# Last pair's experts summed per chosen token on the chip and put out by plain scatters; later expert groups take all images

## The chip, the cores and the metric

The kernel runs on one core of a Trainium2 chip. The metric is the device time of one execution in microseconds (us), lower is better. Engines are named as the profile names them: PE (TensorE, matmul), DVE (VectorE), ACT (ScalarE), POOL (GpSimd), SP (SyncE, which only issues DMAs here). A name with a q ("SPq") is the queue of that engine.

## What is computed

Two layers of a network over 32 images of 56 x 56 tokens with 128 channels: a binarized 3 x 3 convolution and a two-of-eight mixture of experts, then a triangle product and a second expert layer. The change lies in this second expert layer, in which every one of 64 experts chooses 8 tokens of each image:

```python
def _L1_ffn_ref(x, gate_w, gate_b, weight1, weight2):      # x: (32, 3136, 128), layer-normed tokens
    logits = jnp.einsum('bsd,ed->bse', x, gate_w) + gate_b
    probs = jax.nn.softmax(logits, axis=1)                 # over the tokens of an image
    vals, idx = jax.lax.top_k(probs.transpose(0, 2, 1), K) # 8 tokens per expert
    ...
    pooled = jnp.einsum('bked,bke->bed', gathered, topv)
    ...
    h = jax.nn.gelu(jnp.einsum('ebd,edh->ebh', h, weight1), approximate=False)
    ...
    out = jnp.einsum('ebh,eho->ebo', h, weight2)
    out = out.transpose(1, 0, 2)
    weighted = jnp.einsum('beo,bke->bkeo', out, topv).reshape(Bn, K * E, O)
    outputs = jnp.zeros((Bn, Sn, O), dtype=x.dtype)
    outputs = outputs.at[jnp.arange(Bn)[:, None], flat_idx].add(weighted)
    return outputs
# main:  x = x + triangle(ln(x));  t = tokens(x);  t = t + _L1_ffn_ref(_ln_t(t), ...)
```

A token may be chosen by several experts of its image, so the additions of different experts can fall on the same row.

## The kernel before

A first pass over x takes the statistics of the batch norm. The main loop then goes over 16 pairs of images, in 7 units of 896 tokens per pair; pairs overlap. The last stages of a pair are: `tri_out` (the triangle's output added to the tokens `x_`), `gate_turn` (L1045: the finished tokens go to `out` by a DMA from ACT's queue, their norm `yl` to DRAM as `y3_d` by another), `gate_logits`, `top8` (L1090: the eight best tokens per expert, their numbers `near` within the pair and in `pg` within the whole output, their weights in the other half of `pg`, and eight gathers of rows of `y3_d` by POOL) and `pool_rows` (L1141: the weighted sum of the eight rows per expert and image, transposed into `ptc`; for pairs 0 to 14 it goes to `pooled_d` in DRAM; numbers and weights go through DRAM into the tables `picked` and `gains`, one row per image and rank).

The expert matmuls follow when the pooled rows are there, in 16 groups of four experts. `late_experts(last, g)` (L1216) is called twice for each group: with False for pairs 0 to 14 and with True for the last pair, since its pooled rows come latest. A call loads a group's weights (eight loads of 256 KB at L1284 and L1288 and four bias loads of 64 KB at L1239, from SP's queue), and computes all 32 columns of tokens with those of the other pairs at zero: `ph` (first matmul), `hs` (DVE adds the bias), `trh` (transposes), `hG` (ACT, Gelu), `po` (second matmul), a copy by ACT into `oS`, then for each lot `pe` (each image's row repeated eight times by a matmul with `rep`, bias added) and `eo` (DVE, times `gains`, L1358). Then POOL adds it to `out`, one indirect DMA per expert with addition in the DMA (L1375). Lots are images 0 to 15, 16 to 29, 30 to 31; within a lot each of these DMAs waits for the one before it to land, since both may add to the same token, and different lots are declared to be apart. That makes 64 dependent scatters for each of three lots.

Buffers: weights of the experts take turns in the tag `gb` (5 tiles) and in `x` (12 tiles, which also hold tokens and `oS`), `eo` in `xT` (4) for False and `yl` (3) for True, `hs` and `hG` in `u` (5).

The order of the work is not the program's: each stage records operations with an engine, a cost, what it reads and writes, and a rank (the tick in the plan at the end), and `Order.run` (L132) plays them in a model of the engines and writes the instructions of every engine in the order this gave. An engine then takes its instructions strictly in that order, so an instruction that waits holds everything behind it on its engine, DMA issues too.

Of the kernel before, what the change touches and what calls it, by code (L numbers as in the profile page):

```python
# [253 lines left out]
def kernel(ctx: ExitStack, tc: tile.TileContext, a: dict, out: bass.AP):  # L254
# [82 lines left out]


    LOTS = ((0, HB), (HB, B - 2), (B - 2, B))
    picked = [const.tile([HB * K1, E1], I32, name=f"picked_{k}") for k in range(3)]  # L340
    gains = [const.tile([HB * K1, E1], F32, name=f"gains_{k}") for k in range(3)]

    between = const.tile([1, 1], F32, name="between")
    rep = const.tile([B + 1, B * K1], F32, name="rep")
# [24 lines left out]
    with ExitStack() as c2:  # L369
# [35 lines left out]
        def parts(t, n=N7):  # L405
            return [(t, k) for k in range(n)]
# [638 lines left out]
        def gate_turn(p, u):  # L1045

            x_ = live[p]["x", u]

            @op("ACT", 330, r=parts(x_), w=[("out", p, u)], land=1200)
            def _():  # L1050
                ins = nc.scalar.dma_start(out_units[p * NU + u], x_.ap).ins
                apart(ins, lot_of(p))
                stored[lot_of(p)].append(ins.name)

            y = normed(p, u, "ln4", f"yl_{p}_{u}")

            @op("ACT", 330, r=parts(y), w=[("y3", p, u)], land=1200)
            def _():
                nc.scalar.dma_start(units(y3_d[p])[u], y.ap)

            live[p]["yl", u] = copied(turned(y, f"trl_{p}_{u}"), "yl", f"ylT_{p}_{u}")
# [28 lines left out]
        def top8(p):  # L1090

            lg = live[p].pop("lg")
            m8 = new("m8", [2 * E1, K1], f"m8_{p}")
            i8 = new("i8", [2 * E1, K1], f"i8_{p}", U32)
            q = new("sq", [2 * E1, 3], f"sq_{p}")
            pg = live[p]["pg"] = new("pg", [2 * E1, 2 * K1], f"pg_{p}")
            near = new("near", [2 * E1, K1], f"near_{p}", I32)
            all_lg = [(lg, k, i) for k in range(7) for i in range(2)]

            @op("DVE", 3400, r=all_lg, w=[m8])  # L1100
            def _():
                nc.vector.max(m8.ap, lg.ap)

            @op("DVE", 3600, r=all_lg + [m8], w=[i8, q, near, (pg, 0)])
            def _():
                nc.vector.max_index(i8.ap, m8.ap, lg.ap)
                nc.vector.tensor_scalar(q.ap[:, 0:1], m8.ap[:, 0:1], -1.0, None, ALU.mult)
                nc.vector.tensor_scalar(near.ap, i8.ap, row0, None, ALU.add)

                nc.vector.tensor_scalar(  # L1110
                    pg.ap[:, :K1], i8.ap, row0, float(2 * p * S), ALU.add, ALU.add
                )

            @op("ACT", 2700, r=[q, m8], w=all_lg + [(q, 1), (pg, 1)])
            def _():
                nc.scalar.activation(
                    pg.ap[:, K1:], m8.ap, AF.Exp, bias=q.ap[:, 0:1]
                )
                nc.scalar.activation(
                    lg.ap, lg.ap, AF.Exp, bias=q.ap[:, 0:1], accum_out=q.ap[:, 1:2]  # L1120
                )

            @op("DVE", 300, r=[(q, 1), (pg, 1)], w=[(pg, 2)])
            def _():
                nc.vector.reciprocal(q.ap[:, 2:3], q.ap[:, 1:2])
                nc.vector.tensor_scalar(pg.ap[:, K1:], pg.ap[:, K1:], q.ap[:, 2:3], None, ALU.mult)

            for k in range(0, K1, 4):
                rows = live[p]["rows", k // 4] = new("u", [2 * E1, 4, C], f"rows_{p}_{k}")
                for j in range(4):  # L1130
                    @op("POOL", 1300, r=[near] + [("y3", p, u) for u in range(NU)],
                        w=[(rows, j)], land=2600)
                    def _(rows=rows, j=j, k=k):
                        nc.gpsimd.indirect_dma_start(  # L1134
                            out=rows.ap[:, j, :], out_offset=None, in_=y3_d[p],
                            in_offset=bass.IndirectOffsetOnAxis(
                                ap=near.ap[:, k + j : k + j + 1], axis=0
                            ),
                        )

        def pool_rows(p):  # L1141

            pg = live[p]["pg"]
            acc = new("pacc", [2 * E1, C], f"acc_{p}")
            for k in range(K1):
                rows = live[p]["rows", k // 4]

                @op("DVE", 265, r=[(rows, k % 4), (pg, 2)], w=[acc])
                def _(k=k, rows=rows):
                    row, g = rows.ap[:, k % 4, :], pg.ap[:, K1 + k : K1 + k + 1]  # L1150
                    if k == 0:
                        nc.vector.tensor_scalar(acc.ap, row, g, None, ALU.mult)
                    else:
                        nc.vector.scalar_tensor_tensor(
                            acc.ap, row, g, acc.ap, ALU.mult, ALU.add
                        )

            tr = bank(f"tr_p_{p}")
            pt = new("ptc", [C, E1, 2], f"ptc_{p}")
            pk = new("pt", [2 * K1, 2 * E1], f"pt_{p}")  # L1160

            @op("PE", 220, r=[acc, (pg, 0), (pg, 2)], w=[tr])
            def _():
                nc.tensor.transpose(tr.ap[:, :128], acc.ap, ident)
                nc.tensor.transpose(tr.ap[: 2 * K1, 128:256], pg.ap, ident)

            @op("ACT", 300, r=[tr], w=[pt, pk])
            def _():

                nc.scalar.copy(  # L1170
                    pt.ap.rearrange("c e i -> c i e"),
                    tr.ap[:, :128].rearrange("c (i e) -> c i e", i=2),
                )
                nc.scalar.copy(pk.ap, tr.ap[: 2 * K1, 128:256])

            @op("DVE", 100, r=[pk], w=[pk])
            def _():
                nc.vector.tensor_copy(pk.ap[:K1].bitcast(I32), pk.ap[:K1])

            @op("SP", 720, r=[pk], w=[("pick", p)], land=300)  # L1180
            def _():
                for k0, dst, as_ in ((0, pick_d[p], I32), (K1, gain_d[p], F32)):
                    nc.sync.dma_start(
                        dst.rearrange("i k e -> k i e"),
                        pk.ap[k0 : k0 + K1, :].bitcast(as_).rearrange("k (i e) -> k i e", i=2),
                    )

            lot = lot_of(p)

            @op("SP", 720, r=[("pick", p)], w=[("picked", p)], land=300)  # L1190
            def _():
                r0 = (2 * p - LOTS[lot][0]) * K1
                for dst, src in ((picked, pick_d), (gains, gain_d)):
                    nc.sync.dma_start(
                        dst[lot][r0 : r0 + 2 * K1, :], src[p].rearrange("i k e -> (i k) e")
                    )

            if lot == 2:
                live[p]["pt"] = pt
                return  # L1200

            @op("SP", 360, r=[pt], w=[("pooled", p)], land=1500)
            def _():
                nc.sync.dma_start(
                    pooled_d[:, :, p, :], pt.ap.rearrange("c (g e) i -> c g (e i)", e=NE)
                )
# [3 lines left out]

        tokens_out = out.rearrange("b h w c -> (b h w) c")
        last_out = {}

        def late_experts(last, g):  # L1216

            name = f"{last}_{g}"
            es = slice(g * NE, (g + 1) * NE)
            n = (NP - 1) * NE * 2  # L1220

# [23 lines left out]
                    a["L1_ffn_weight2"][es, HID, :].unsqueeze(0),  # L1245
                )

            if last:
                pt = live[NP - 1]["pt"]

                @op("DVE", 250, r=[pt], w=[(oS, "t")])
                def _():
                    nc.vector.memset(tok(), 0.0)
# [1 line left out]
            else:  # L1255
# [3 lines left out]
                        pool(), pooled_d[:, g, : NP - 1, :].rearrange("c p x -> c (p x)")  # L1259
                    )  # L1260

                @op("DVE", 300, r=[(oS, "p")], w=[(oS, "t")])
                def _():
                    nc.vector.memset(tok()[:, :, NP - 1, :], 0.0)
                    nc.vector.tensor_copy(
                        tok()[:, :, : NP - 1, :],
                        pool().rearrange("c (p e i) -> c e p i", e=NE, i=2),
# [70 lines left out]
            def _():  # L1338
                nc.scalar.copy(flat(oS)[:B, : NE * C], po.ap[:B])

            for lot in (2,) if last else (0, 1):
                i0, i1 = LOTS[lot]
                rows = (i1 - i0) * K1
                pe = bank(f"pe_{name}_{lot}")
                eo = new("yl" if last else "xT", [128, N7, C], f"eo_{name}_{lot}")

                @op("PE", 870, r=[(oS, "o"), (oS, "b")], w=[pe])
                def _(pe=pe, i0=i0, i1=i1, rows=rows):
# [14 lines left out]
                for j in range(NE):  # L1363
# [6 lines left out]
                    def _(j=j, eo=eo, lot=lot, rows=rows):  # L1370
# [13 lines left out]
                            tc.add_manual_dep(ins, before_, sync, reason="adds to the same tokens")  # L1384
                        apart(ins, lot)
                        last_out[lot] = [ins.name]

        sync = mybir.DependencyInfo(mybir.DependencyClass.Sync, mybir.DependencyReason.DATA)

# [241 lines left out]
        def put(tick, stage, *args):  # L1631
            plan.append((args[0] * PERIOD + tick, len(plan), stage, args))

        def late(tick, last, g):
            plan.append(((NP - 1) * PERIOD + tick, len(plan), late_experts, (last, g)))

        def before(tick, stage, *args):
            plan.append((tick - 4 * NUT, len(plan), stage, args))
# [42 lines left out]
            put(t + 3.83, top8, p)  # L1681
            put(t + 7, pool_rows, p)
        for g in range(E1 // NE):
            late(t + 7.5 - PERIOD + 1.15 * g, False, g)
            late(t + 7.5 + g, True, g)
        for tick, _, stage, args in sorted(plan, key=lambda e: e[:2]):
            op.rank = tick
            stage(*args)
# [42 lines left out]
```

## Time and profile before

| | us |
|---|---|
| Median of 3 runs (4117.01 to 4127.04) | 4121.77 |
| The profiled execution | 4114.83 |
| its span, first to last instruction | 4113.1 |
| PE busy (share of the span) | 3723.7 (91%) |
| DVE busy | 3148.4 (77%) |
| ACT busy | 2355.4 (57%) |
| POOL busy | 480.7 (12%) |
| Chain that ended last: PE / DMA / ACT / DVE | 63% / 12% / 11% / 7% |
| Issues of weight loads, `w_False` and `w_True` | 128 and 128, 256 KB each |
| Scatters `out<-eo_False,picked`, `out<-eo_True,picked` | 128 and 64 |

How to read it: busy times are those of instructions that compute; waiting and DMA issue don't count. The "chain that ended last" is followed back from the last instruction, at each step to what released it. A group of instructions is named by line, engine, and output<-inputs. "DMA share" is the mean busy share of the core's 16 DMA engines; "granted clock" is the share of full speed that PE got. In a table by stretches the columns are the stretch, its length, the busy times of PE, PE's weight loads, DVE, ACT and POOL with instruction counts, then granted clock, DMA share and GB/s.

### The profile page before, as it was taken

To read this page: it belongs to the slowest core of one execution; us is meant where nothing else is said; L and a number is where in the kernel's file an instruction comes from. 1 tells how busy PE (TensorE), PEld (TensorE's weight loads), DVE (VectorE), ACT (ScalarE), POOL (GpSimd) and SP (SyncE) were. 2 spreads that over 40 slices of the span, in tenths; PEclk is the share of its full clock that TensorE was granted. 3 is DMA by queue.
4 is the path that set the end of the run, shared out by engine and by line. 5 is a ranking of instruction groups with operands and counts; after the bars stand their busy time and mean duration, and the time that the engine had idled before them with its cause. 6 is when DMAs were issued, how large, how long until landed. Compare 5 with 4: busy or idle time off the path is not lost.

```text
span 4113.1 us, 78868 instructions
## 1 busy us (share of the span) xinstructions
PE 3723.7 (91%) x28012; PEld 2922.3 (71%) x28012; DVE 3148.4 (77%) x10300; ACT 2355.4 (57%) x5474; POOL 480.7 (12%) x537
## 2 busy tenths in 40 slices
PE   7998999999999999999999999999999999896661
PEld 6886877777877787777777777777777777654341
DVE  7997888788888888888888888888888888652110
ACT  5996256565656565656565756575757565552010
POOL 1000001010100010101000101010001010046664
PEclk9999999999999999999999999999999999897775
DMA  7996646464645464655555555555555555577880
GB/s 254 353 347 214 224 152 232 147 239 149 236 172 212 165 222 168 218 184 201 188 196 187 199 191 194 192 194 203 182 192 193 195 190 194 179 205 205 210 224 13
DMA packets 324889, 824.16 MB, mean 200 GB/s; under 512 B 73856, under 2 KB 99088, under 8 KB 324496
## 3 DMA queue, kind: packets, MB, share of 16 engines
q1 hardware_dynamic: 260848, 696.32, 48.9%
q10 hardware_dynamic: 40096, 105.99, 6.6%
q0 software_dynamic: 23552, 16.80, 2.9%
q8 instruction: 223, 3.65, 0.4%
q14 instruction: 170, 1.39, 0.1%
HBM read 652.04 MB, written 166.85 MB: 199 GB/s over the span
## 4 chain that ended last, share of the span: by engine, by line
PE 63%; DMA 12%; ACT 11%; DVE 7%; issue 3%; POOL 3%; SPq 1%; ACTq 0%; POOLq 0%; DVEq 0%
PE acc L790 30%; PE ps_cv L591 6%; DMA out<-eo_False,picked 4%; PE gram L1441 3%; PE ps_g L988 3%; DMA out<-eo_True,picked 2%; DMA gb<-gate 2%; PE ps_zo L1016 2%; ACT yt L520 2%; PE ps_l L1075 2%; PE ps_b L835 2%; PE tr L435 2%; POOL out L1375 2%; DMA rows<-y,near 2%; PE tro L435 2%
## 5 line engine op out<-in xcount | busy, mean ns | idle before, releaser
L790 PEld LDWEIGHTS acc<-expert_w,gb 128*128 128x128 f32 x12544 | 1444.7, 195 | 102.6 <-DVE gb L785 34.2
L790 PE MATMUL acc<-expert_w,gb 128*128 128x128 f32 x12544 | 1469.1, 279 | 50.4 <-DVE gb L785 38.2
L785 DVE TENSOR_TENSOR gb<-gb,xT 128x1024 f32<-128x1024 f32 x784 | 944.1, 1220 | 80.8 <-DMA gb<-gate 71.1
L446 DVE BATCH_NORM_STATS2 stln<-x 128x6 f32<-128x128 f32 x2352 | 589.0, 285 | 2.4
L1134 POOL DMA_INDIRECT rows<-y,near x128 | 184.0, 1438 | 3391.3 <-PE trm L435 1902.4
L591 PE MATMUL ps_cv<-frame,w_sign 128*128 128x448 bf16 x2016 | 418.4, 355 | 7.1 <-DVE frame L569 7.1
L520 ACT ACTIVATE yt<-x,rmln 128x128 f32<-128x128 f32 x784 | 322.5, 484 | 159.2 <-DVE rmln L505 155.8
L520 ACT ACTIVATE ym<-x,rmln 128x128 f32<-128x128 f32 x784 | 326.6, 490 | 97.1 <-DVE rmln L508 83.6
L520 ACT ACTIVATE yl<-x,rmln 128x128 f32<-128x128 f32 x784 | 326.6, 486 | 35.6 <-DVE rmln L505 20.4
L591 PEld LDWEIGHTS <-w_sign 128*128 128x128 bf16 x2016 | 193.3, 97 | 185.2 <-issue 20.1
L599 ACT ACTIVATE cv<-ps_cv,cv_shift,cv_scale 128x448 f32<-128x448 f32 x224 | 161.6, 724 | 98.7 <-PE ps_cv L591 92.6
L541 ACT COPY xT<-trm 128x512 f32<-128x512 f32 x224 | 112.1, 541 | 179.7 <-PE trm L435 145.9
L1375 POOL DMA_INDIRECT out<-eo_False,picked x128 | 195.0, 1524 | 148.3 <-DMA out<-eo_False,picked 67.4
L520 ACT ACTIVATE y<-x,rm 128x128 f32<-128x128 f32 x448 | 195.3, 491 | 23.5 <-DVE rm L505 11.7
L541 ACT COPY ylT<-trl 128x512 f32<-128x512 f32 x224 | 111.5, 535 | 157.7 <-PE trl L435 140.3
L1441 PE MATMUL gram<-y 128*128 128x128 f32 x1568 | 199.1, 280 | 0.0
L988 PE MATMUL ps_g<-yT,wg 128*128 128x448 f32 x448 | 198.8, 552 | 0.0
L802 DVE TENSOR_TENSOR x<-acc,x 128x512 f32<-128x512 f32 x224 | 139.2, 621 | 77.0 <-PE acc L790 76.6
L446 DVE BATCH_NORM_STATS2 st<-x 128x6 f32<-128x128 f32 x784 | 180.6, 282 | 20.3 <-DMA x<-in_x 20.1
L1441 PEld LDWEIGHTS gram<-y 128*128 128x128 f32 x1568 | 195.5, 201 | 0.0
L1026 DVE SCALAR_TENSOR_TENSOR sg<-ps_zo,bz,sg 128x448 f32<-128x448 f32 x224 | 150.0, 679 | 43.8 <-PE ps_zo L1016 41.0
L998 ACT ACTIVATE sg<-ps_g,bg 128x448 f32<-128x448 f32 x224 | 137.5, 634 | 68.6 <-PE ps_g L988 39.2
(217 smaller groups left out, 5645.3 us busy)
## 6 DMA issues: line engine op xcount, KB each, us to landing
gb<-gate SPq DMA_DIRECT2D x784, 512.0 KB
x<-in_x SPq DMA_DIRECT2D x224, 448.0 KB
y<-yT SPq DMA_DIRECT2D x112, 448.0 KB
ys<-y SPq DMA_DIRECT2D x112, 448.0 KB
out<-x ACTq DMA_DIRECT2D x112, 448.0 KB
y<-yl ACTq DMA_DIRECT2D x112, 448.0 KB
w_False<-in_L_ffn_weight SPq DMA_DIRECT2D x128, 256.0 KB
w_True<-in_L_ffn_weight SPq DMA_DIRECT2D x128, 256.0 KB
```

Of the source, the lines that this page charges most:

```text
L435: nc.tensor.transpose(ps.ap[:, n * 128 : (n + 1) * 128], get()[:, n0 + n, :], ident)
L446: nc.vector.bn_stats(st.ap[:, c0 + k, :], src.ap[:, k, :])
L520: nc.scalar.activation(dst.ap[:, k, :], src.ap[:, k, :], AF.Identity, bias=m, scale=r)
L541: nc.scalar.copy(t.ap[:, n0 : n0 + k, :].rearrange("c n p -> c (n p)"), ps.ap[:, : k * 128],)
L591: nc.tensor.matmul(acc, lhsT=w_sign[:, tap, :], rhs=frames[f][:, 8 * band + kh : 8 * band + kh + 8, kw : kw + W], start=(tap == 0), stop=( ...
L599: nc.scalar.activation(cv.ap[:, :, 64 * h : 64 * h + 64], ps.ap[:, :448].rearrange("c (q n) -> c n q", n=N7), AF.Identity, bias=cv_shift, ...
L785: nc.vector.tensor_tensor(gb.ap, gb.ap, over(xT.ap[:, n, :], E0), ALU.mult)
L790: nc.tensor.matmul(acc.ap[:, n % 4 * C : (n % 4 + 1) * C], lhsT=gb.ap[:, e, :], rhs=expert_w[:, e * C : (e + 1) * C], start=(e == 0), stop ...
L988: nc.tensor.matmul(psg.ap[:, :448], lhsT=wg, rhs=yT[:, H * img + r0 : H * img + r0 + 8, :].rearrange("c r w -> c (r w)"), start=True, stop ...
L1134: nc.gpsimd.indirect_dma_start(out=rows.ap[:, j, :], out_offset=None, in_=y3_d[p], in_offset=bass.IndirectOffsetOnAxis(ap=near.ap[:, k + j ...
L1375: ins = nc.gpsimd.indirect_dma_start(out=tokens_out, out_offset=bass.IndirectOffsetOnAxis(ap=picked[lot][:rows, e : e + 1], axis=0), in_=e ...
L1441: nc.tensor.matmul(gram.ap[:, :C], lhsT=y.ap[:, n, :], rhs=y.ap[:, n, :], start=(g % G16 == 0 and n == 0), stop=(g % G16 == G16 - 1 and n ...
```

## The change

The last pair (lot 2) loses its accumulating scatters. Instead, what each chosen token of it is to become is worked out whole: for each choice (expert, rank) the output of every expert that chose the same token is summed, each with its weight, by a matmul with a matrix of choices; the token itself, gathered from a copy in DRAM, is added; and eight plain scatters (one per rank, 128 rows each) write the finished rows over those in `out`. Choices of the same token write the same row with the same content.

For that `gate_turn` stores the last pair's tokens a second time into `x_last_d`; `top8` makes `at`, the row numbers in the output as integers; `pool_rows` leaves out the last pair's tables; `late_experts` stores the two rows of the last pair into `o_last_d` and drops its third lot; `last_sums` builds the matrix of choices and gathers the tokens; `last_out_rows` does the matmuls and the scatters. And groups 10 to 15 (`LATE = 10`) run once, later, with the last pair's tokens among the columns, instead of twice; groups 0 to 9 still run twice. In the plan the second runs come at half the former distance.

```diff
+    x_last_d = dram.tile([2 * S, C], F32, name="x_last_d")
+    near_d = dram.tile([2 * E1, K1], F32, name="near_d")
+    o_last_d = dram.tile([2, E1, C], F32, name="o_last_d")
...
@@ gate_turn
+            if p == NP - 1:
+                @op("ACT", 330, r=parts(x_), w=[("x_last", u)], land=1200)
+                def _():
+                    nc.scalar.dma_start(units(x_last_d)[u], x_.ap)
...
@@ late_experts
-        def late_experts(last, g):
+        LATE = 10
+        def late_experts(alone, g):
+            with_last = alone or g >= LATE
...
-                @op("DVE", 300, r=[(oS, "p")], w=[(oS, "t")])
+                @op("DVE", 300, r=[(oS, "p")] + with_last * [pt], w=[(oS, "t")])
                 def _():
-                    nc.vector.memset(tok()[:, :, NP - 1, :], 0.0)
+                    if with_last:
+                        nc.vector.tensor_copy(tok()[:, :, NP - 1, :], pt.ap[:, es, :])
...
-            for lot in (2,) if last else (0, 1):
+            if with_last:
+                @op("SP", 360, r=[(oS, "o")], w=[("o_last", g)], land=200)
+                def _():
+                    nc.sync.dma_start(
+                        o_last_d[:, es, :].rearrange("i e c -> i (e c)"),
+                        flat(oS)[B - 2 : B, : NE * C],
+                    )
+            for lot in () if alone else (0, 1):
...
+        def last_sums():
+            pg, near, at = (live[NP - 1][k] for k in ("pg", "near", "at"))
+            nums, t, m = (new("yl", [128, N7, C], f"last_{k}") for k in ("nums", "t", "m"))
...
+            @op("SP", 360, r=[(pg, 0)], w=["near_d"], land=300)
+            def _():
+                nc.sync.dma_start(near_d, pg.ap[:, :K1])
+            @op("SP", 720, r=["near_d"], w=[nums], land=300)
...
+            for k in range(K1):
+                @op("DVE", 600, r=[nums, (pg, 0), (pg, 2)], w=[m if k == 0 else t])
+                def _(k=k):
+                    nc.vector.tensor_scalar(
+                        (t_ if k else m_)(), nums_(), pg.ap[:, k : k + 1],
+                        pg.ap[:, K1 + k : K1 + k + 1], ALU.is_equal, ALU.mult,
+                    )
+                if k:
+                    @op("DVE", 600, r=[t], w=[m])
+                    def _():
+                        nc.vector.tensor_tensor(m_(), m_(), t_(), ALU.add)
+            for h in range(2):
+                rows.append(new("x", [128, N7, C], f"last_rows_{h}"))
+                for j in range(4):
...
+                        nc.gpsimd.memset(between, 0.0)
+                        nc.gpsimd.indirect_dma_start(
+                            out=rows[h].ap[:, j, :], out_offset=None, in_=x_last_d,
+                            in_offset=bass.IndirectOffsetOnAxis(ap=near.ap[:, k : k + 1], axis=0),
+                        )
+        def last_out_rows():
+            o = new("u", [128, N7, C], "last_o")
+            @op("SP", 1440, r=[("o_last", g) for g in range(E1 // NE)], w=[o], land=300)
+            def _():
+                nc.sync.dma_start(o.ap[:, 0, :], o_last_d.rearrange("i e c -> (i e) c"))
...
+                            nc.tensor.matmul(
+                                ps.ap[r, j * C : (j + 1) * C], lhsT=by_choice[r, 4 * h + j, :],
+                                rhs=o.ap[r, 0, :], start=True, stop=True,
+                            )
...
+                    nc.vector.tensor_tensor(flat, ps.ap, flat, ALU.add)
...
+                        ins = nc.gpsimd.indirect_dma_start(
+                            out=tokens_out,
+                            out_offset=bass.IndirectOffsetOnAxis(ap=at.ap[:, k : k + 1], axis=0),
+                            in_=rows[h].ap[:, j, :], in_offset=None,
+                        ).ins
+                        for before_ in last_out.get(2, stored[2]):
+                            tc.add_manual_dep(ins, before_, sync, reason="the same tokens")
+                        apart(ins, 2)
+                        last_out[2] = [ins.name]
...
@@ the plan
         for g in range(E1 // NE):
-            late(t + 7.5 - PERIOD + 1.15 * g, False, g)
-            late(t + 7.5 + g, True, g)
+            late(
+                t + (7.5 - PERIOD + 1.15 * g if g < LATE else 7.1 + 1.15 * (g - LATE)),
+                late_experts, False, g,
+            )
+            if g < LATE:
+                late(t + 7.5 + 0.5 * g, late_experts, True, g)
+        late(t + 7.4, last_sums)
+        late(t + 14, last_out_rows)
```

## The prediction

> **What bounds the kernel now.** I read the page first (shares, the slices, the chain by line), then the busy times by stretches of the end, then the chain of waits of the last 600 us in order of time, then the landing times and start times of single groups of instructions. The profiled execution took 4114.83 us: the span of 4113.1 and 1.7 around it. The change touches only what happens after about 3600 us: in the order of each engine's instructions the first difference is the last pair's output stage (about 3640 us of this trace).
>
> From the page (busy tenths of 40 slices; a slice is 103 us):
> ```profile
> PE   7998999999999999999999999999999999896661
>
> DMA  7996646464645464655555555555555555577880
> ```
> In the last three or four slices PE falls to 6 and 1 and POOL, idle before, is busy: the end is not the body's regime. By stretches, with granted clock, DMA share and GB/s last:
> ```profile
> 3750.00:3792.00 42.00, 25.31 (x136) 17.23 (x136) 8.10 (x21) 3.93 (x8) 32.41 (x39) 0.72 0.71 178
> ...
> 3836.00:3923.00 87.00, 57.46 (x326) 38.52 (x326) 14.65 (x35) 8.02 (x14) 68.36 (x93) 0.75 0.77 187
> 3923.00:3970.00 47.00, 31.52 (x191) 20.48 (x186) 7.19 (x17) 4.88 (x9) 34.72 (x48) 0.84 0.98 276
> ...
> 4031.00:4113.00 82.00, 1.43 (x6) 0.24 (x4) 2.71 (x4) 0.57 (x1) 33.27 (x49) 0.53 0.07 3
> ```
> The reader is to see two things: a stretch in which the DMA engines are full (0.98, 276 GB/s), and a last 82 us in which nothing works (DMA 0.07). The chain of waits says what that is (start, us, what):
> ```profile
> 3972.32 1.56 POOL out L1375
> 3974.19 1.48 POOL out L1375
> 3975.98 2.71 DMA out<-eo_True,picked
> 3978.95 3.56 DMA out<-eo_True,picked
> ...
> 4095.15 2.58 DMA out<-eo_True,picked
> 4098.00 2.62 DMA out<-eo_True,picked
> 4100.89 1.30 POOL out L1375
> ```
> From 3975.98 to 4103.75 the last pair's scatters follow one another, 40 of the 64, each waiting until the one before has landed: 127.8 us over 39 steps, 3.28 each. Before that the chain is the other lots' scatters, two chains side by side. Their landing times, first of `eo_False`, then of `eo_True`:
> ```profile
> DMA to landing us min/median/max: 3.1/4.7/7.7
> ```
> ```profile
> DMA to landing us min/median/max: 2.6/2.7/7.2
> ```
> And the pace of the expert groups, in ScalarE's Gelu instructions:
> ```profile
> 3767.70 0.60 ACT L1324 ACTIVATE hG_False<-trh_False 128x512 f32<-128x512 f32 x1 [2.93 <-PE trh_False L1317]
> ...
> 4027.07 0.60 ACT L1324 ACTIVATE hG_True<-trh_True 128x512 f32<-128x512 f32 x1 [2.00 <-PE trh_True L1317]
> ```
> That is group 10 of `False` to group 15 of `True`: 21 intervals in 259.4 us, 12.35 each.
>
> **What the Trainium skill says.** "DMA: Bandwidth & Descriptors", "Anatomy of one DMA", gives a fixed cost of about 2.0 us, most of it the receipt of the write; the trace's smallest scatters (16 rows) take 2.6, so a chain of small dependent scatters costs what its count says, not its bytes. The same page, "Issuing engines are not separate DMA queues": stores from ScalarE, loads from SP and scatters from GpSimd share 16 engines. The trace agrees: 128-row scatters land in 3.1 us at best and 7.7 at worst, and the share is 0.91 in 3656 to 3750. The same page, "Rules for kernel authors": a plain scatter that names a row twice keeps one writer's data; the new scatters repeat rows, always with equal values, and no run here shows that case yet. "TensorE: Matmul & The Clock Gate", first part, says that idle windows of some 3.4 us halve the clock; the stretches at 0.72 to 0.84 agree, and 32 matmuls of `po` take 3.6 or 5.3 us accordingly.
>
> **The change, part by part.**
> Removed: 64 accumulating scatters of lot 2 with 64 memsets, 16 `pe`/`eo` steps of it, the reload of weights for groups 10 to 15 (6 of 32 groups), and the last pair's pick and gain tables (SP stood 11.0 us at L1183 for them).
>
> x_last stores: 7 of 448 KB, 3.2 MB, from ScalarE's queue, each behind a store of the same tile. At the 258 GB/s of 3656 to 3750 that is 12 us of DMA time, in a stretch where the chain is scatters' landing. Bounds 0 and 12; I take 3, since that stage's 94 us are only partly DMA's.
>
> Choice matrix: 8 comparisons and 7 additions of 128x512 on VectorE. An addition takes 0.69 (the row of `hs`), a comparison 0.69 at most, 0.42 by an estimate from "VectorE: DVE Perf Modes" ("The perf-mode tier table", 1227 ns for 2048 elements of fp32 in SBUF). Sum 8.2 to 10.3 us, between 3754 and 3795, where VectorE is busy 8.1 of 42 us. It hides behind the row gathers, which land some 5 us apart. What remains: four accumulations of 0.35 stand behind the last gather instead of one, 1 us on `ptc`. Its table goes through DRAM, so SP waits about 2.5 us in one place before group 9's third weights; nobody needs group 10 before `ptc` at 3791, so nothing.
>
> Gathers of x: 8 more on GpSimd, about 2.1 us each with memset (1.03, 0.48, gaps 0.27 and 0.3). They stand between groups 8's and 9's scatters as the pooled rows stand between 6's and 7's: there eight rounds took 3750.44 to 3792.82, 5.3 each, and twelve rounds without them 3684.73 to 3748.85, also 5.3. Nothing.
>
> Groups 10 to 15 with all images: group 10 now waits for `ptc` (3791) where it ran at 3768. Its scatters' turn comes at about 3836, after groups 8 and 9, and its `eo` is due at about 3808 (one group's time on PE, 7 to 9 us, doubled since `True` 0 is woven in). No loss. But from here all of the remaining groups come after 3791: 10, `True` 0 to 9, 11 to 15. Weights for 10, `True` 0 and half of `True` 1 fit in the buffers by then. The buffers come free with group 10's `po`, about 3804, so 13.5 groups have to be loaded after 3804.
>
> Time per group is the number that decides. A group is 8 x 256 KB of weights and 4 x 64 KB of bias, 2.36 MB: at 276 GB/s 8.6 us. In the full stretch the bias loads start at 3916.09 and, five groups later, 3963.34: 9.45 each, scatters beside them. Upper bound 12.35 from the Gelu rows, where VectorE was stopped in front of `eo` waiting for the scatters of both kinds; the `True` ones are gone. Two things cost anew: `last_rows` holds two of twelve `x` buffers to the end (a group uses five), and each `o_last` store stands in SP's queue ahead of later weights, until its group's copy. I take 10.4.
> 3804 + 3 + 13.5 x 10.4 = 3947; the last weight lands 2 later; `po`, its copy, `pe` and `eo` 5.3 + 0.6 + 2.0 + 0.7, with gaps 9: group 15's `eo` at 3958.
> Scatters are not later: 20 rounds from 3840 at 5.0 (4.7 landing and 0.3) give 3940.
> The tail then: three rounds of group 15 in a DMA that grows idle, 3.9 each; the first plain scatter before the fourth round (its `o` goes to DRAM and back, about 10 us after the copy, and is there); then seven in a chain at 3.3 (3.1 for 128 rows without load, bounds 2.9 and 5.0). The last starts at 3958 + 11.7 + 3 + 20 = 3993. The span ended 9.4 after the last scatter's start; with 128 rows 10: 4003.
> Against its own 4113.1 that is 110 less. The runs' median is 6.9 above the profiled execution; 110 off 4121.8 gives 4012.
>
> **The rivals.**
> Late weights: SP's waits and ten buffers keep the pace at the old 12.35. For it: SP already waited 41.1 us for `po_True` at L1284 in this stretch. Against: most of that followed from VectorE's wait on `True` scatters. 13.5 x 1.95 = 26 us more: 4038.
> Scatters the bound: weights at 8.6 put `eo` at 3933, and group 15's scatters wait for their turn at about 3940: 18 less, 3994. For it: 276 GB/s was reached. Against: only for 47 us.
> Slower: SP's queue goes into lock step. If each `o_last` store blocks the loads behind it until its group is computed, load (9.4) and compute with store (7 to 10) no longer overlap, up to 19.7 per group: 3804 + 266 + 2 + 9 + 45 = 4126, 13 more, 4135. It decides from (4113 - 3860) / 13.5 = 18.7 on. Against: the store of one group stands behind three quarters of the next one's loads, and often a further group's, so two groups are always under way.
>
> **How the numbers follow.** Forecast 50 in 100, late weights 25, scatters the bound 15, something between 4060 and 4113 for a wait I don't see 6, lock step 4. Likeliest 4012. The range 3985 to 4050 takes in the second and third and leaves about 15 outside. A difference under 0.2% (8 us) couldn't be told from none here; so faster 0.95, same 0.01, slower 0.04.
>
> **What would show it.** No `eo_True` and no L1358-like step for lot 2; the last scatter of group 15 near 3970; eight plain scatters about 3.3 apart in a chain; bias loads some 10.4 apart from 3810 to 3940, with a DMA share above 0.9. Wrong would be: a share of 0.75 there (late weights), VectorE waiting for scatters in front of `eo` for groups 13 to 15 (scatters the bound), SP waiting for ScalarE's copy at the `o_last` stores for over 5 us each (lock step), or plain scatters of 5 us.

## The result, and the profile after

The changed kernel takes 4010.27 us (median of 4 runs, 4003.43 to 4013.14) against 4122.47 for the kernel before in the same comparison: ratio 0.9726, 95% interval 0.9709 to 0.9743, some 113 us less. A second comparison gave 0.9717 (0.9695 to 0.9739). The prediction was 4012. The profiled execution took 4013.14, its span 4011.4.

The body differs between the two profiled executions by no work, only by drift, so I count from the first gather of pair 14's pooled rows (POOL, 3563.24 in the trace before, 3570.05 after), which lies ahead of everything that the change touches. From there to the end it was 549.9 us, and is 441.4: 108.5 less.

POOL in the page's 40 slices, in the kernel before and then in the changed one with PE and DMA beside it:
```profile
POOL 1000001010100010101000101010001010046664
```
```profile
PE   6998999999999999999999999999999999988574
...
POOL 1000000101010001010101010101000101004655
...
DMA  7996546373746464645555555555555555457685
```
The last slice was PE 1 and DMA 0; it is now PE 4 and DMA 5. Half of the 82 us in which hardly anything worked are left: 41 us in which only POOL and its DMAs work. By stretches (length, busy PE, its weight loads, DVE, ACT, POOL, then granted clock, DMA share, GB/s):
```profile
3656.00:3750.00 94.00, 67.83 (x409) 39.66 (x409) 33.61 (x129) 42.95 (x89) 46.39 (x61) 0.86 0.92 265
...
3792.00:3836.00 44.00, 16.91 (x105) 10.58 (x105) 7.21 (x20) 2.88 (x6) 32.42 (x46) 0.66 0.63 147
3836.00:3923.00 87.00, 69.14 (x447) 48.28 (x448) 12.93 (x32) 11.39 (x20) 45.30 (x61) 0.92 0.91 261
3923.00:3970.00 47.00, 33.54 (x210) 22.78 (x208) 7.80 (x16) 4.68 (x8) 27.38 (x37) 0.89 0.71 176
3970.00:4011.00 41.00, 0.00 (x0) 0.00 (x0) 0.00 (x0) 0.00 (x0) 23.92 (x35) 0.53 0.22 29
```
In 3836 to 3923 the DMA engines are now full (0.91, 261 GB/s, where it was 0.77 and 187). Ahead of that there is a hole of 44 us at 0.63, and after 3970 only POOL works. The chain of waits shows what ends last:
```profile
3880.21 6.36 DMA w_True<-in_L_ffn_weight
...
3907.87 8.27 DMA out<-eo_False,picked
...
3935.97 7.24 DMA out<-eo_False,picked
...
3974.25 0.69 POOL out L1417
...
3990.21 2.29 DMA out<-last_rows,at_last
3992.49 0.27 issue
3992.76 2.24 DMA out<-last_rows,at_last
```
Up to 3907 the chain runs through weights (`w_True`) and the engines that use them. From 3907.87 on it is the scatters of lots 0 and 1, first their landing (7 to 8 us in the lines shown), after 3952 mostly POOL's issuing, and at last the plain scatters. So at the end it is not the weights that are late. What POOL issues there:
```profile
3971.79 1.49 POOL L1417 DMA_INDIRECT out<-eo_False,picked  x1 [0.27 <-issue]
...
3974.25 1.55 POOL L1417 DMA_INDIRECT out<-eo_False,picked  x1 [0.93 <-issue]
...
3985.22 1.00 POOL L1530 DMA_INDIRECT out<-last_rows,at_last  x1 [0.27 <-issue]
...
4005.70 0.96 POOL L1530 DMA_INDIRECT out<-last_rows,at_last  x1 [1.44 <-DMA out<-last_rows,at_last]
```
The scatter of 3974.25 is the first of group 15; its `eo` had been ready since 3960.7, and the last sums since 3969 (DVE L1519 at 3968.30 for 0.69). They waited for their turn in POOL's order.

### The profile page after: what moved, and what is told of

The parts are those of the page before. It is cut to its first block, busy times and chain, and to the rows that moved or that the text cites. A ratio compares the mean times of both kernels' runs of the same rounds, so it can differ in the third digit from the quotient of the medians.

```text
span 4011.4 us, 78057 instructions
## 1 busy us (share of the span) xinstructions
PE 3678.5 (92%) x27747; PEld 2896.2 (72%) x27747; DVE 3143.3 (78%) x10284; ACT 2348.2 (59%) x5461; POOL 418.2 (10%) x441
## 4 chain that ended last, share of the span: by engine, by line
PE 65%; ACT 10%; DMA 10%; DVE 8%; POOL 3%; issue 3%; SPq 1%; ACTq 0%; POOLq 0%; DVEq 0%
PE acc L794 31%; PE ps_cv L595 6%; DMA out<-eo_False,picked 4%; PE gram L1593 3%; PE ps_g L992 2%; PE ps_zo L1020 2%; PE ps_b L839 2%; PE ps_l L1084 2%; DMA rows<-y,near 2%; PE tr L439 2%; DMA gb<-gate 2%; ACT yt L524 2%; PE tro L439 2%; DVE gb L789 2%; PE trm L439 2%
## 6 DMA issues: line engine op xcount, KB each, us to landing
x<-in_x SPq DMA_DIRECT2D x224, 448.0 KB
y<-yT SPq DMA_DIRECT2D x112, 448.0 KB
ys<-y SPq DMA_DIRECT2D x112, 448.0 KB
out<-x ACTq DMA_DIRECT2D x112, 448.0 KB
y<-yl ACTq DMA_DIRECT2D x112, 448.0 KB
```

## Two theories

Predicted was that the loads of weights after the last pair's pooled rows set the end: this is W. The trace speaks for another, S: the two chains of dependent scatters, of lots 0 and 1 (64 scatters each; one of each lot make a round), set the end, and the loads come in time. Both kinds share the DMA engines and, through the four `eo` buffers, DVE, so the experiments change one of them at a time.

The table gives every run: ratio to the kernel before on the same chip with its interval, and five moments of the profiled execution, counted from the first gather of pair 14's pooled rows: the last pair's table `ptc`, the last Gelu of a group, the last scatter of lots 0 and 1, the first plain scatter, the end.

| kernel | ratio (95%) | ptc | last Gelu | last of lots 0, 1 | first plain | end |
|---|---|---|---|---|---|---|
| before | 1 | 227.7 | 463.8 | 411.0 | none | 549.9 |
| changed | 0.9726 (0.9709-0.9743) | 235.3 | 383.8 | 418.4 | 415.2 | 441.4 |
| changed, again | 0.9717 (0.9695-0.9739) | 235.1 | 383.6 | 414.7 | 411.5 | 437.7 |
| LATE 16 | 0.9799 (0.9783-0.9815) | 239.5 | 439.0 | 419.7 | 452.4 | 476.1 |
| LATE 12 | 0.9739 (0.9715-0.9763) | 238.3 | 410.9 | 413.3 | 424.3 | 448.0 |
| LATE 8 | 0.9719 (0.9696-0.9742) | 229.6 | 372.3 | 428.8 | 405.7 | 441.3 |
| late scatters left out | 0.9671 (0.9651-0.9690) | 236.0 | 378.7 | 281.9 | 392.2 | 419.1 |
| `True` left out | 0.9600 (0.9573-0.9628) | 233.1 | 296.7 | 385.7 | 325.3 | 392.0 |
| rows from `out` | 0.9700 (0.9675-0.9725) | 232.7 | 382.3 | 415.1 | 412.0 | 438.1 |
| gathers first | 0.9688 (0.9672-0.9704) | 209.6 | 376.8 | 409.6 | 406.4 | 432.5 |
| both of these | 0.9702 (0.9677-0.9726) | 202.6 | 371.6 | 403.2 | 400.0 | 426.2 |
| both, LATE 8 | 0.9658 (0.9630-0.9685) | 200.6 | 346.2 | 408.4 | 385.3 | 420.8 |

(The kernel before with the later groups alone follows below.) The ratios of four runs are good to some 0.2%, 8 to 10 us; the moments come from one execution each, and in the two traces of the unaltered changed kernel the scatter chain and the end differ by 4.

## The experiments

**The two parts apart.** The matrix and the plain scatters alone, with all 16 groups run twice as before:
```diff
-        LATE = 10
+        LATE = 16
-        late(t + 14, last_out_rows)
+        late(t + 16, last_out_rows)
```


> LATE = 16: the sums by the matrix of choices and the plain scatters alone, every group still runs twice (six more groups of weights than in the changed kernel, 4010 us). Theory W (the loads of weights after the pooled rows are there set the end): groups 10 to 12 come before the pooled rows as in the kernel before, 19 groups follow instead of 16, and each costs 9.2 us: 28 to 55 us more, 4038 to 4065. Theory S (the two chains of dependent scatters of lots 0 and 1 set the end, loads only through the landing times): the chains keep their 64 rounds and the loads use up the slack beside them first: 4010 to 4030.

Measured 4048.88, ratio 0.9799: some 83 us less than before, and 30 more than with LATE 10. Here W holds. Its POOL timeline:
```profile
3985.16 1.49 POOL L1417 DMA_INDIRECT out<-eo_False,picked  x1 [0.99 <-DMA out<-eo_False,picked]
...
4017.78 1.00 POOL L1530 DMA_INDIRECT out<-last_rows,at_last  x1 [31.10 <-DVE last_rows L1519]
```
The scatters of lots 0 and 1 are over at 3985, and POOL stands idle for 31.1 us until the last sums come. The later groups alone, in the kernel before with its accumulating scatters of lot 2 kept:
```diff
+        LATE = 10
-            for lot in (2,) if last else (0, 1):
+            for lot in (2,) if last else (0, 1, 2) if with_last else (0, 1):
-            late(t + 7.5 + g, True, g)
+            if g < 10:
+                late(t + 7.5 + 0.5 * g, True, g)
```


> The kernel before with its accumulating scatters for lot 2, but groups 10 to 15 run once with all images: the late groups alone. Both theories: lot 2 still has 64 dependent additions that can't start before about 3820; about half are done beside the other lots' scatters until 3990, the rest follow at 3.3 us: 4080 to 4110, a gain of 10 to 40. If the fewer loads were what brought the gain, it would be 4060 or less.

Measured 4106.84, ratio 0.9936 (0.9914 to 0.9958), some 26 us less; in the profiled execution it was 11. The last third of its chain of waits:
```profile
4081.45 0.27 issue
4081.72 2.60 DMA out<-eo_True,picked
4084.32 0.27 issue
4084.59 2.73 DMA out<-eo_True,picked
...
4094.18 2.78 DMA out<-eo_False,picked
```
Lot 2's accumulating scatters still follow one another one by one, some 2.9 us apart, so fewer weight loads help little. Most of the gain comes from taking these scatters away; the 26 and the 83 add up, within their intervals, to the 113 of both.

**Without the late scatters.** Lots 0 and 1 of groups 10 to 15 are computed and not scattered:
```diff
-                for j in range(NE):
+                for j in range(NE if g < LATE else 0):
```


> The changed kernel with the scatters of lots 0 and 1 of groups 10 to 15 left out (48 of 128; those experts' outputs are missing for images 0 to 29), all else computed. W: the loads still run until 3950 and the end moves only by the rounds behind the last eo: 4000 to 4008. S: the end falls back to the path of the loads, the last pair's sums at about 3968 in the trace of the changed kernel, then eight plain scatters at 2.6 and 6: 3985 to 3996.

Measured 3998.67, ratio 0.9671, about 21 us below the changed kernel (0.0051 from the mean of its two ratios, 0.9722, as in all such differences below). S expected 14 to 25 us below the 4010 of the changed kernel, W 2 to 10: by the difference S holds. The microseconds alone fall between the two ranges, since the kernel before took 4133.57 beside this run, 11 more than beside the changed one. POOL now waits for the sums, which come 23 us sooner than the plain scatters' turn came in the changed kernel:
```profile
3861.02 1.50 POOL L1417 DMA_INDIRECT out<-eo_False,picked  x1 [0.84 <-DMA out<-eo_False,picked]
...
3971.36 1.00 POOL L1530 DMA_INDIRECT out<-last_rows,at_last  x1 [108.81 <-DVE last_rows L1519]
```
Of the 23, 16.3 are the time that the sums had waited (398.9 to 415.2 in the changed kernel's count), and 5 more are there at the last Gelu already, since the loads run faster without scatters (378.7 instead of 383.8). So the loads' path had about 16 us of slack: at LATE 10 the loads did not set the end.

**Without the `True` groups.** Ten of the late groups are neither loaded nor computed, and the last pair's experts 0 to 39 are missing from the sums:
```diff
+                nc.vector.memset(o.ap[:, 0, :], 0.0)
...
-            if g < LATE:
-                late(t + 7.5 + 0.5 * g, late_experts, True, g)
```


> The changed kernel with the `True` groups left out: the last pair's experts 0 to 39 are not computed, their rows are zero, and their weights (10 of the 15 or so late groups) are not loaded. All scatters of lots 0 and 1 and the eight plain ones stay. If W were right alone, the end would come as much sooner as ten groups at 9.3 us, up to 90 us less. S says that the chain of 64 rounds of scatters stays; only its landing times shorten, because the DMA engines are no longer full: from group 10's first scatter to group 15's first 20 rounds at 3.7 to 4.6 us (74 to 92) instead of 116.6, so 25 to 42 us less, ratio 0.962 to 0.967.

Measured 3960.32, ratio 0.9600: 50 us below the changed kernel, between what W expected alone (90) and what I gave S (25 to 42). The chain of lots 0 and 1 ends 29 to 33 us sooner, within S's range; what I had left out is that the plain scatters then all lie between those of lots 0 and 1, so that the tail after these (23 us from the last of them to the end in the changed kernel) shrinks to 6. POOL's timeline in this run:
```profile
3885.32 1.49 POOL L1417 DMA_INDIRECT out<-eo_False,picked  x1 [0.27 <-DVE eo_False L1400]
...
3887.11 1.55 POOL L1417 DMA_INDIRECT out<-eo_False,picked  x1 [0.27 <-DMA out<-eo_False,picked]
...
3888.96 1.49 POOL L1417 DMA_INDIRECT out<-eo_False,picked  x1 [0.27 <-issue]
```
Two scatters take 3.64 us, the two issues and the gaps (1.55 + 1.49 + 2 x 0.27 = 3.58; the rest is the ends of the two memsets): a round of these instructions can't be shorter on POOL. With most of the loads gone the median landing in 3857 to 3950 is 3.3, where it is 5.9 in the changed kernel, and POOL's issuing becomes the pace from 3875 on. This run's waits, summed from 3791 on (us, times, longest), show where the backlog goes:
```profile
DVE eo_False L1400 <- DMA out<-eo_False,picked: 86.4, 14, 19.1
```
VectorE stood 86.4 us in front of `eo`, since the scatters had not emptied a buffer; the matmuls were done early (last Gelu at 297) and the scatters were the bound.

**The stores of x.** The rows of the last pair's tokens are gathered from `out`, where `gate_turn` puts them anyway, and the seven extra stores are left out:
```diff
-                    nc.scalar.dma_start(units(x_last_d)[u], x_.ap)
...
-                            out=rows[h].ap[:, j, :], out_offset=None, in_=x_last_d,
-                            in_offset=bass.IndirectOffsetOnAxis(ap=near.ap[:, k : k + 1], axis=0),
+                            out=rows[h].ap[:, j, :], out_offset=None, in_=tokens_out,
+                            in_offset=bass.IndirectOffsetOnAxis(ap=at.ap[:, k : k + 1], axis=0),
```


> The changed kernel without its x_last stores: the rows of the last pair's tokens are gathered from `out`, where they were stored anyway. The seven stores of 448 KB went from ScalarE's queue in the 130 us ahead of the pooled-row gathers, where the two kernels' traces differ by 6.3 us. If the stores are that difference, the table `ptc` of the last pair comes some 6 us sooner after the first gather of pair 14 (about 229 instead of 235). W (the late loads set the end) and S (the scatters of lots 0 and 1 set it) then both say 3 to 8 us less in all, ratio to the kernel before 0.971 to 0.972, since both start from that stage. If the 6.3 us are not the stores, no change (0.9726).

Measured 4005.51, ratio 0.9700; `ptc` comes 2.5 us sooner than in the changed kernel's two traces (232.7 after 235.3 and 235.1), not 6. The interval overlaps with theirs, so a gain at the end is not shown. The same stage, from the first scatter to the first pooled-row gather, took 133.5 and 131.6 us in the changed kernel's two traces and 130.2 here; 127.2 before. Over all traces in which the gathers keep their place it was 130.1 to 134.3 in seven with the stores (mean 132.2) and 127.2 to 130.2 in three without them (129.2): some 3 us, with a spread as large.

**The last pair's gathers first.** In the changed kernel the eight gathers of the last pair's pooled rows alternate with rounds of the older groups' scatters. Here they go ahead:
```diff
+            op.rank -= 20 * (p == NP - 1)
```


> The changed kernel with the last pair's eight gathers of pooled rows put ahead of group 6's scatters on POOL, back to back, instead of one between every two scatters. The pooled rows then come some 25 to 30 us sooner. W: the loads follow, the end comes 15 to 30 us sooner: 3980 to 3995. S: the scatters wait for up to 11 us of gathers and nothing else changes: 4005 to 4022.

Measured 4002.47, ratio 0.9688 (0.9672 to 0.9704), some 14 us less; the interval touches that of the changed kernel's second comparison, so the gain is only just shown. W expected 15 to 30 less, S hardly any (4005 to 4022). `ptc` comes 26 us sooner, but the last Gelu only 7 and the first plain scatter 9. DVE again stood up to 15.2 us in front of `eo` for the scatters of older groups, and the groups behind it waited. Neither theory has this: the start of the loads and the chain of scatters are coupled. Both edits together, with the rows gathered from `out` as above:

> Both edits: the last pair's pooled-row gathers ahead of the older groups' scatters (which alone gave ratio 0.9688), and no x_last stores (rows gathered from `out`). The two act in different stretches, so they should add: 3 to 8 us less than that run, ratio 0.967 to 0.968. If the scatters of lots 0 and 1, pushed later by the gathers, are by now the only bound (S), what `ptc` gains does not arrive at the end, and the ratio is 0.9685 to 0.969.

Measured 3998.81, ratio 0.9702 (0.9677 to 0.9726). That is above both expectations (0.967 to 0.968, and 0.9685 to 0.969), with an interval that takes them in. The profiled execution is 6 us shorter than with the gathers alone, the runs don't show it: their intervals overlap, and a gain of the second edit isn't shown.

**LATE 8 and 12, the changed kernel beside them.** The unaltered changed kernel as the yardstick:

> The changed kernel again, unaltered, on the chip of the two runs beside it, as their yardstick and to see how far its stages repeat. Both W (the late loads set the end) and S (the scatters of lots 0 and 1 set it) expect the ratio 0.971 to 0.974 again, the table `ptc` 235 +- 2 us after the first gather of pair 14, the last scatter of lots 0 and 1 418 +- 5 after it, and rounds of 5.6 to 6.0 us from group 10's first scatter to group 15's.

Measured 0.9717, with `ptc` at 235.1, the chain's last scatter at 414.7 and rounds of 5.75 from group 10's first to group 15's (285.5 to 400.5). Then two groups fewer to load twice:
```diff
-        LATE = 10
+        LATE = 8
-        late(t + 14, last_out_rows)
+        late(t + 16, last_out_rows)
```


> The changed kernel with LATE = 8 alone (two groups fewer are loaded twice; groups 8 and 9 wait for `ptc`), the last sums two ticks later. W: two groups of 9.3 us less, 12 to 18 us faster than the run of the changed kernel beside it. S: the loads don't matter as long as they come in time; groups 8 and 9 scatter later than now, since `ptc` holds them, and the chain ends no sooner: 0 to 10 us slower. The run with LATE = 8 and the gathers ahead was 0.9658; if LATE does that, this one is 0.966 to 0.968, if the gathers do it, 0.972 or more.

Measured 0.9719, no difference to 0.9717. The loads do come sooner (last Gelu at 372.3, 11 sooner), and nothing of it arrives: groups 8 and 9 now wait for `ptc`, and the chain of scatters ends 10 to 14 later. Its ACT timeline and its stretches:
```profile
3746.24 0.60 ACT L1358 ACTIVATE hG_False<-trh_False 128x512 f32<-128x512 f32 x1 [16.73 <-PE trh_False L1351]
3794.95 0.27 ACT L1186 COPY ptc<-tr_p 128x128 f32<-128x128 f32 x1 [41.31 <-PE tr_p L1182]
3800.16 0.60 ACT L1358 ACTIVATE hG_False<-trh_False 128x512 f32<-128x512 f32 x1 [3.64 <-PE trh_False L1351]
```
```profile
3740.00:3800.00 60.00, 14.04 (x61) 7.95 (x61) 23.96 (x44) 7.20 (x8) 49.74 (x62) 0.56 0.44 74
```
No group is computed for 54 us, and the DMA engines are 0.44 busy. That is S. And the other way:
```diff
-        LATE = 10
+        LATE = 12
```


> The changed kernel with LATE = 12 alone (two more groups are loaded twice). With LATE = 16 it was 30 us over LATE = 10, with the loads as the bound, so the two curves cross in between. S holds at 10, with some 17 us of slack on the loads: two more groups of 9.3 us use it up, so 0 to 6 us slower than LATE = 10, ratio 0.973 to 0.975. If W held at 10 already: 15 to 19 slower, ratio 0.976 to 0.978.

Measured 0.9739, 9 us over the yardstick by the ratio (its interval overlaps): within S's range for the ratio, between the two (0 to 6 and 15 to 19) in microseconds. Here the last scatter of lots 0 and 1 starts at 413.3, POOL then waits 9.45 us for the sums, and the plain scatters follow from 424.3. So in these traces the loads bind at 12 and the scatters at 10, and the two lines cross in between.

**Gathers first and LATE 8.** The kernel with both edits of above and LATE 8:

> The former kernel with LATE = 8 (two groups fewer are loaded twice; groups 8 and 9 wait for `ptc` too) and the last sums put two ticks later. W: two groups of 9.3 us less to load, up to 18 us less, ratio 0.963 to 0.964. S: the loads weren't the bound, and groups 8 and 9 now start their scatters later, so the chain of rounds is late by what POOL idles: 0 to 15 us more than without it, ratio 0.968 to 0.972.

Measured 3984.11, ratio 0.9658 (0.9630 to 0.9685): this beats both kernels, about 26 us below the changed one (0.0064 of 4122), whose two intervals it does not touch. It lies between what W and S expected by the ratio; below the run with both edits it is 18 us, the most that W allowed, but those two intervals overlap. LATE 8 by itself gave nothing, for `ptc` held groups 8 and 9. With `ptc` at 200.6 it holds them less: the time without a Gelu of a group is 32 us (3740.96 to 3773.31) instead of 54, and the last scatter of lots 0 and 1 comes 20 sooner than with LATE 8 alone. Its stretches:
```profile
3836.00:3910.00 74.00, 60.00 (x364) 39.86 (x364) 11.09 (x26) 9.03 (x16) 37.79 (x49) 0.91 0.95 267
3910.00:3950.00 40.00, 12.39 (x72) 9.36 (x72) 5.64 (x9) 1.17 (x2) 31.91 (x42) 0.60 0.36 35
```
The loads are done at 3910 (DMA share from 0.95 to 0.36); from then on the scatters land quickly, POOL issues without pause (31.9 of 40 us), and five of the eight plain scatters fall between those of lots 0 and 1.

Not tried: plain scatters without the chain among them, since scatters of the same rows would then be under way together; and more buffers for `eo`.

## Why the prediction was right, and where it was not

The time was right to 2 us, in part by luck. Counted from the common start, predicted was an end at 4003 - 3563.2 = 439.8; it came at 441.4. The terms, by the prediction's own steps:

**The loads: right.** Predicted were 13.5 groups at 10.4 us each from 3807, the last weight at 3947. SP's timeline in the changed kernel (bias loads of groups, and the last weight):
```profile
3811.60 1.72 SPq L1271 DMA_DIRECT2D hs_False<-in_L_ffn_weight  x4
...
3819.59 2.61 SPq L1271 DMA_DIRECT2D hs_True<-in_L_ffn_weight  x4
...
3844.49 2.78 SPq L1271 DMA_DIRECT2D hs_True<-in_L_ffn_weight  x4
...
3936.92 3.83 SPq L1271 DMA_DIRECT2D hs_False<-in_L_ffn_weight  x4
...
3946.42 0.33 SPq L1322 DMA_DIRECT2D w_False<-in_L_ffn_weight  x1
```
From group 11 to group 15 there are twelve intervals in 125.3 us, 10.44 each, and the last weight is issued at 3946.4. But the 10.44 is a mean of unlike things: ten intervals after 3844 at 9.24, between the 8.6 and the 9.45 that the prediction named, one of 8.0, and one of 24.9. In that one DVE stood in front of group 10's `eo`, by the waits of the changed kernel from 3791 on:
```profile
DVE eo_False L1400 <- DMA last_rows<-x_last_d,near: 15.6, 1, 15.6
```
The profile names the landing of a gather, the last thing to come; but the `eo` buffers come free with group 8's scatters, the last of which was issued at 3827.23 just ahead of it. The second trace of the changed kernel names these for its stop of 16.4:
```profile
DVE eo_False L1400 <- DMA out<-eo_False,picked: 24.4, 5, 16.4
```
That group 10 brings no loss was wrong by that one stop, and the price per group hid it. `eo` of group 15 then was ready at 3960.7, predicted 3958, in a trace whose body is 6.8 later: 4 sooner than predicted.

**The scatters: wrong.** "Scatters are not later: 20 rounds from 3840 at 5.0 (4.7 landing and 0.3) give 3940" is the step that failed. They ran from 3857.7 to 3974.2, 5.83 each. The later start of 17.6 is 6.8 of drift, 6.3 in the stage that ends at the pooled-row gathers, 4.1 from there on, and 0.4. The term that was mis-sized in the pace is the landing. 4.7 is the median over the whole kernel before, with and without loads beside the scatters, while the forecast itself put a DMA share above 0.9 beside these rounds. The landing times of `eo_False` by stretch: before in 3656 to 3750 (DMA share 0.91), in 3923 to 3970 (0.98) and in the 20 rounds (3840 to 3956, 0.86), changed in 3857 to 3950 (0.95) and in 3951 to 3990:
```profile
DMA to landing us min/median/max: 3.1/5.9/7.7
...
DMA to landing us min/median/max: 3.8/4.8/5.5
...
DMA to landing us min/median/max: 3.1/4.7/7.6
...
DMA to landing us min/median/max: 3.4/5.9/8.3
...
DMA to landing us min/median/max: 3.1/3.2/3.9
```
The changed kernel's first 14 rounds, with the loads beside them (273 GB/s), took 6.58 each, and the last six 4.07; the second trace has 6.31 and 4.44, with a median landing of 6.1 beside the loads. That loads beside them lengthen the landings is shown, by this and by the 3.3 without the `True` groups. But the DMA share alone doesn't tell by how much: the trace before has 5.9 at 0.91 and 4.8 at 0.98, so it would have given a range, 5.1 to 6.2 per round, and what makes the difference stays open. By an estimate from these numbers 5.9 and 0.3 make 6.2; for the rest, the two lots take turns in POOL's order, so a late landing of one can hold up the other, which no run tests.

Counting the starts in the kernel before would have given 5.80 each (276.9 to 392.9), the right number for another reason. A round there held a third scatter, of lot 2, and nine of the 20 rounds took 5.26 to 5.29, POOL issuing one after the other:
```profile
3897.26 1.56 POOL L1375 DMA_INDIRECT out<-eo_False,picked  x1 [0.27 <-issue]
...
3899.12 1.48 POOL L1375 DMA_INDIRECT out<-eo_False,picked  x1 [0.27 <-issue]
...
3900.91 1.31 POOL L1375 DMA_INDIRECT out<-eo_True,picked  x1 [0.27 <-issue]
...
3902.52 1.56 POOL L1375 DMA_INDIRECT out<-eo_False,picked  x1 [0.27 <-issue]
```
The change took that third scatter away, and the landings, with more loads beside them (273 GB/s where it was 224), grew by as much.

So group 15 waited 13.6 us for its turn, which the forecast did not have, and at the end the rival "scatters the bound" held in its mechanism, though not in its price of 3994, which rested on the same 3940. The sign that I had named for it, VectorE waiting for scatters in front of `eo` for groups 13 to 15, did not show: the work stood in POOL's order instead.

**The tail: too dear.** From group 15's first scatter to the last plain one I had 34.7 (11.7, 3 and 20), measured 31.5; from there to the end 10, measured 5.7. The plain scatters follow each other every 2.5 us, not 3.3. Together 7.6 too much.

So 4.1 less, 13.6 more and 7.6 less make 1.9 more, of which the forecast's rounding up to 4003 takes 0.3: the total stood because terms of opposite sign nearly cancelled. That is luck.

**x_last stores.** Taken at 3 (bounds 0 and 12): the stage grew by 4.4 and 6.3 in two traces, and `ptc` came 2.5 sooner without them. The price was right as far as it can be told. `ptc` itself came 7.6 and 7.4 later, where 4 were in the sum (3 and the four accumulations, whose 1 measured 0.9).

**The rest.** The x gathers: the eight rounds with them took 6.2 each (3808.04 to 3857.68; 6.0 in the second trace), not the 5.3 taken. But the same rounds took 5.9 in the kernel before, without gathers (3792.82 to 3840.18), so at most 0.3 to 2.3 us in all are theirs. (The twelve rounds without gathers that the prediction put at 5.3 took 5.5: they end at 3750.44, and 3748.85 is the start of a gather.) The choice matrix took VectorE 9.2 us, within the 8.2 to 10.3: comparisons 0.53 to 0.55 us each, where the estimate was 0.42. SP stood 12.8 us in front of its table, not 2.5, but group 9 was still computed at 3781.8, 51 us ahead of its first scatter. The lock step of SP didn't come: SP waited 7.4 and 4.2 us, once each, at the `o_last` stores. Late weights at 12.35 per group didn't come either; at LATE 16 the loads did set the end, at 10.7 per group (bias loads from 3807.2 to 3978.2, 16 intervals).

On the Trainium skill: "DMA: Bandwidth & Descriptors", "Anatomy of one DMA", fits a DMA as 2.0 us and its bytes over 436 GB/s, for these 64 KB an estimate of 2.15. The plain scatters landed in 2.2 at the least, which agrees. The same section calls descriptor generation small; in these traces POOL is busy 1.5 us for each accumulating scatter, and that is what set the pace of the rounds from 3952 to 3985. How much of it is that generation the trace doesn't say.

## What to carry to other kernels

Where several dependent chains of small DMAs run beside full loads, take the landing time from stretches with such loads beside them, as a range (here 4.8 to 5.9), not the median over the kernel. A pace read from starts holds only while the same thing sets it: ask for each round in the trace whether a landing or the issuing engine did. A stage with two lines, loads and scatters, can hide either's error: price both to their end, and see which waits. An edit that relieves one of them (fewer loads) pays only once what feeds the other (here the table that groups 8 and 9 wait for) is early enough.

## What the hardware did that I had not expected

An accumulating scatter of a group's 112 or 128 rows lands in 3.1 us at best and in 8.4 at worst, and a plain one of 128 rows in 2.2 (landing times of `eo_False` and of the last rows in the changed kernel):
```profile
DMA to landing us min/median/max: 3.1/4.7/8.4
```
```profile
DMA to landing us min/median/max: 2.2/2.4/4.9
```
Beside the full loads the accumulating ones take nearly twice as long as after them, 5.9 and 3.2 by the medians of the changed kernel above; yet in the kernel before it was 4.8 in its fullest stretch. POOL takes mostly 1.49 to 1.56 us to issue an accumulating one and 0.96 to 1.0 for a plain one. So two chains side by side did not go faster than 3.64 us per round with their 1 x 1 memsets in between, which the run without the `True` groups shows, and the end of the changed kernel nearly (3.66).
